# Attention half steps of a decoder kernel reordered: maxima transposed in the next half step, bias additions ahead of the maximum, output projection in odd half steps

## The chip, the cores and the metric

The kernel runs on one core of one Trainium2 chip. The metric is the device time of one execution in microseconds (us); lower is better. A kernel's time is the median of its runs.

## What is computed

The input is `x` of 64 sequences x 128 positions x 256 features, a context `ctx` of the same shape, and a mask of 64 x 128 ones and zeros. Six residual sublayers follow one another, each on the layernorm of the sum so far:

```python
x = x + window_attention(layernorm(x), ...)            # A
x = x + cross_attention_0(layernorm(x), ctx, mask)     # B, its attention
x = x + slot_network(layernorm(x), ...)                # B, beside it
x = x + self_attention_with_bias(layernorm(x), ...)    # D
x = x + cross_attention_1(layernorm(x), ctx, ...)      # E
x = x + bitnet_feed_forward(layernorm(x), ...)         # F
```

What matters here are the three full attentions (B, D and E). Each has 16 heads of 16 features and, for each sequence, computes

```python
scores = einsum('bhqd,bhkd->bhqk', q, k) * scale (+ bias)   # 128 x 128 for each head
p      = softmax(scores, axis=-1)
y      = einsum('bhqk,bhkd->bhqd', p, v)                    # then the output projection
```

In B, `q` and `k` are slices of the normalised `x` and of the context, without a projection, and the mask is applied to queries and keys. In D there is a learned bias for each head, query and key, which is minus infinity where the key comes after the query. In E queries come from `x`, keys and values from `ctx`, all projected. The slot network routes each token to the best 8 of 64 slots (top 8, softmax), averages the tokens of each slot, updates the slots with a gated cell, and reads them back.

## The kernel before

**Stages.** The core runs A, B, D, E, F in turn (B holds the first cross attention and the slot network). `x` stays in SBUF, in 16 groups of GB = 4 sequences ("batches" in the code, 64 in all). The three attentions share one function, `attention_stage`, which is software-pipelined in half steps. Half step `j` belongs to batch `n = j // 2` and half `hf = j % 2`; a half is two of the four row groups of heads, thus 8 heads.

**One batch's way through the half steps.** Since the sums and the weighted values want keys on the partitions, and the maximum wants queries there, the scores of each half are computed twice: once as they are (`first`, for the maximum over keys) and, three half steps later, transposed and with the maximum already taken from the query (`second`, for the exponential).

- `score_burst` (L396, matmuls L409) issues 32 small matmuls when both jobs are there: 16 of `first` and 16 of `second`, alternating, into one PSUM tile `sc` of four banks. This pool has one buffer, so a burst can start only when the last reader of the burst before is done.
- `score_max` (L416) takes the `first` half: in D it adds the bias into an SBUF tile (`sb`, L422), then the negated maximum over keys goes to `negmax` (L424), on DVE.
- `score_exp` (L430) takes the `second` half: in D it adds the bias (`e`, L436, DVE) and takes the exponential of `e`; in B and E the exponential reads the PSUM tile itself (L438, ACT).
- `shift_query` (L442): four PE transposes (L447) of `negmax`, when both halves of the batch are there, then a DVE addition (L451) gives `q2`, the query with the maximum subtracted by way of an extra feature. `second` uses `q2`: half 0 of batch n at half step 2n+3.
- `weigh_values` (L454): 16 matmuls (L459) with the exponentials, copied by ACT (L464). `divide` (L467): four transposes (L471), reciprocal (L474) and product (L478) on DVE. `turn_output` (L483): two transposes (L488) and an ACT copy (L490). `finish_batch` (L493): the output projection (L140) and the addition to `x` by `fin` (L1053 in D and E, L623 in B, DVE).

The loop at the end of `attention_stage` places these: the batch's `weigh_values` at lag 5 from its first half step, `divide` at lag 6, `turn_output` at 7, `finish_batch` at 8, `shift_query` at lag 1. `start(n + 1)` calls the stage's `prep` for the next batch in even half steps. PSUM tiles of all the other steps come from a pool of four buffers (`ps`).

**Around it.** In D and E the projections of the next group (`group_project`) are a generator in nine portions: layernorm; transposes; four portions of two matmuls into q and k (L131, ACT copies L1009); two portions of values (L1020, DVE additions L1025). `advance(g + 1, 2)` in `prep` takes two portions for each batch, in the even half step. In E the layernorm portion also issues the context's DMA on SP's queue. In B `prep` builds padded queries and keys on DVE and POOL and transposes them (L616), and the `tick` of the slot network, called at the end of every half step, takes one portion of `slots_route` or of two `slots_update` generators; a group's routing starts at the half step behind the one in which its last batch is finished.

**Order.** The program is written as one sequence; a scheduler then fixes the order of each engine's instructions, and each engine works through its own list. So where a function stands in the loop influences, but does not alone decide, where its instructions stand on PE, DVE, ACT and POOL.

Of the kernel before, what the change touches and what calls it, by code (L numbers as in the profile page):

```python
# [10 lines left out]
F = mybir.dt.float32  # L11
BF = mybir.dt.bfloat16
AF = mybir.ActivationFunctionType
ALU = mybir.AluOpType
AX = mybir.AxisListType
# [4 lines left out]
S = 128  # L20
WIN = 7
SLOTS = 64
GB = 4
# [389 lines left out]
    return t  # L413


def score_max(k, pool, t, job, bias_s):  # L416
    nc = k.nc
    b, hf = job
    src = t[:, 0:2, :]
    if bias_s is not None:  # L420
        sb = pool.tile([S, 2, 512], F, tag="sb", name="sb")
        nc.vector.tensor_tensor(sb, src, bias_s[:, hf * 2 : hf * 2 + 2, :], ALU.add)  # L422
        src = sb
    nc.vector.tensor_reduce(  # L424
        b.lay.extra(b.nm, hf * 2),
        src.rearrange("p r (c m) -> p r c m", m=S), AX.X, ALU.max, negate=True,
    )


def score_exp(k, pool, w1, t, job, bias_t):  # L430
    nc = k.nc
    b, hf = job
    src = t[:, 2:4, :]
    e = (w1 if hf else pool).tile([S, 2, 512], F, tag=f"e{hf}", name=f"e{hf}")
    if bias_t is not None:
        nc.vector.tensor_tensor(e, src, bias_t[:, hf * 2 : hf * 2 + 2, :], ALU.add)  # L436
        src = e
    nc.scalar.activation(e, src, AF.Exp)  # L438
    b.e[hf] = e


def shift_query(k, pool, b):  # L442
# [11 lines left out]
def weigh_values(k, pool, b):  # L454
    nc = k.nc
    av = psum(k)
    for c in range(4):
        for r in range(4):
            nc.tensor.matmul(  # L459
                av[32 * r : 32 * r + 32, c * S : (c + 1) * S], b.va[:, b.lay.head(c, r), :],  # L460
                b.e[r // 2][:, r % 2, c * S : (c + 1) * S], start=True, stop=True,
            )
    b.avs = pool.tile([128, 4, S], F, tag="avs", name="avs")
    nc.scalar.copy(b.avs, av.rearrange("p (c l) -> p c l", l=S))  # L464


def divide(k, pool, b):  # L467
    nc = k.nc
    tv = psum(k)
    for c in range(4):  # L470
        nc.tensor.transpose(tv[:, c * S : (c + 1) * S], b.avs[:, c, :], k.ident)  # L471
    avv = tv.rearrange("p (h i) -> p h i", i=32)
    rec = pool.tile([S, H], F, tag="rec", name="rec")
    nc.vector.reciprocal(rec, avv[:, :, 16])  # L474
    if b.row_scale is not None:
        nc.vector.tensor_scalar(rec, rec, b.row_scale, None, ALU.mult)
    b.ao = pool.tile([S, H, DH], F, tag="ao", name="ao")
    nc.vector.tensor_tensor(  # L478
        b.ao, avv[:, :, 0:16], rec.unsqueeze(2).to_broadcast([S, H, DH]), ALU.mult
    )  # L480
# [12 lines left out]
def finish_batch(k, b, wo):  # L493
    py = psum(k)
    out_project(k, py[:, 0:D], b.aT, wo)
    b.fin(py[:, 0:D])


def attention_stage(k, pool, w1, prep, wo, lay, bias_s=None, bias_t=None, tick=None):

    nms = []
    for i in range(2):
        t = w1.tile([S, lay.size], F, name=f"negmax{i}")
        k.nc.gpsimd.memset(t, 0.0)
        nms.append(t)
    bs = {}  # L510

    def start(n):
        b = bs[n] = prep(n)
        b.lay = lay
        b.nm = nms[n % 2]
        b.e = [None, None]

    def at(j, lag):
        n, odd = divmod(j - lag, 2)
        return bs.get(n) if not odd else None  # L520

    start(0)
    for j in range(2 * k.NB + 9):
        n, hf = divmod(j, 2)
        first = (bs[n], hf) if n < k.NB else None
        m, mf = divmod(j - 3, 2)
        second = (bs[m], mf) if 0 <= m < k.NB else None
        if first or second:
            t = score_burst(k, first, second)
            if first:  # L530
                score_max(k, w1, t, first, bias_s)
            if second:
                score_exp(k, pool, w1, t, second, bias_t)
        if at(j, 5):
            weigh_values(k, pool, at(j, 5))
        if at(j, 6):
            divide(k, pool, at(j, 6))
        if at(j, 7):
            turn_output(k, pool, at(j, 7))
        if at(j, 8):  # L540
            finish_batch(k, bs.pop((j - 8) // 2), wo)
        if hf == 0 and n + 1 < k.NB:
            start(n + 1)
        if hf == 1 and n < k.NB:
            shift_query(k, pool, bs[n])
        if tick is not None:
            tick(j)

# [421 lines left out]
def stage_attn(k, w, cross, bias=None):  # L970
    nc = k.nc
    pre = "we" if cross else "wd"
    bias_t, bias_s = bias if bias is not None else (None, None)
    with k.tc.tile_pool(name=pre, bufs=2) as wp, k.tc.tile_pool(name=pre + "1", bufs=1) as w1:
        vas = []
        for i in range(2):
            va = w1.tile([S, GB, H, 32], F, name=f"{pre}va{i}")
            nc.gpsimd.memset(va, 0.0)
            nc.gpsimd.memset(va[:, :, :, 16:17], 1.0)
            vas.append(va)  # L980
        proj, pending = {}, {}

        def group_project(g):

            xn = w1.tile([S, GB, D], F, tag="xn", name="xn")
            cx = load_group(k, w1, g) if cross else None
            layernorm(k, wp, g, xn)
            nc.gpsimd.tensor_tensor(  # L988
                k.x[g], k.x[g], w.bo.unsqueeze(1).to_broadcast([S, GB, D]), ALU.add
            )  # L990
            yield
            xnT = w1.tile([128, 2, GB * S], F, tag="xnT", name="xnT")
            transpose_group(k, xn, xnT)
            if cross:
                kvT = w1.tile([128, 2, GB * S], F, tag="kvT", name="kvT")
                transpose_group(k, cx, kvT)
            else:
                kvT = xnT
            yield
            qt = wp.tile([128, 4, GB * S], F, tag="qt", name="qt")  # L1000
            kt = wp.tile([128, 4, GB * S], F, tag="kt", name="kt")
            for dst, wt, src, sc, bi in (
                (qt, w.wq, xnT, w.parq, w.bq), (kt, w.wk, kvT, w.par, w.bk)
            ):
                for cc in range(2):
                    p = psum(k)
                    project(k, p, wt, cc * 128, 128, src, 0, GB * S)
                    for par in range(2):
                        nc.scalar.activation(  # L1009
                            dst[:, 2 * cc + par], p, AF.Identity,  # L1010
                            scale=sc[:, par : par + 1], bias=bi[:, cc, par : par + 1],
                        )
                    yield
            va = vas[g % 2]
            for b2 in range(2):
                p = psum(k)
                for j in range(2):
                    b = b2 * 2 + j
                    for kc in range(2):
                        nc.tensor.matmul(  # L1020
                            p[:, j * D : (j + 1) * D], kvT[:, kc, b * S : (b + 1) * S],
                            w.wv[:, kc, :], start=(kc == 0), stop=(kc == 1),
                        )
                for j in range(2):
                    nc.vector.tensor_tensor(  # L1025
                        va[:, b2 * 2 + j, :, 0:DH],
                        p[:, j * D : (j + 1) * D].rearrange("p (h d) -> p h d", d=DH),
                        w.bv.rearrange("p (h d) -> p h d", d=DH), ALU.add,
                    )
                if b2 == 0:  # L1030
                    yield
            proj[g] = qt, kt, va

        def advance(g, parts):
            for _ in range(parts):
                if g in pending and next(pending[g], pending) is pending:
                    del pending[g]

        def prep(bi):
            g, b = divmod(bi, GB)  # L1040
            if bi == 0:
                pending[0] = group_project(0)
            if b == 0:
                advance(g, 9)
                if g + 1 < k.G:
                    pending[g + 1] = group_project(g + 1)
            advance(g + 1, 2)
            qt, kt, va = proj[g]
            t = Batch()
            t.qt, t.kt = qt[:, :, b * S : (b + 1) * S], kt[:, :, b * S : (b + 1) * S]  # L1050
            t.va, t.row_scale = va[:, b], None
            xb = k.x[g][:, b, :]
            t.fin = lambda y: nc.vector.tensor_tensor(xb, y, xb, ALU.add)  # L1053
            return t

        attention_stage(k, wp, w1, prep, w.wo, Heads(True), bias_s, bias_t)

# [375 lines left out]
```

## Time and profile before

| | |
|---|---|
| three runs (us) | 3784.18, 3775.18, 3778.06; median 3778.06 |
| the profiled execution (us) | 3773.99, its span 3772.2 |
| mean granted PE clock | 0.89 |
| PE busy | 2993.5 us, 79% of the span |
| DVE busy | 2562.4 us, 68% |
| ACT busy | 1274.6 us, 34% |
| POOL busy | 1058.7 us, 28% |
| chain that ended last | PE 47%, DVE 32%, POOL 10%, ACT 7%, issue 3%, DMA 1% |

By the timeline stage A takes the first 608 us, B 614 to 1560 (with the preparation of D's bias to about 1655), D 1658 to 2420, E 2430 to 3100 and F the rest. "Busy" counts neither register work nor the issue of DMAs. PE is TensorE's matmuls, PEld its weight loads, DVE the vector engine, ACT the scalar engine, POOL the general engine, SP the queue that starts most DMAs. In the chain of waits, a line `PE x <- DVE y: a, b, c` means that PE stood before x for a us in all, b times, the longest c, and that y released it. In the chain that ended last a line gives start, duration, engine, output and line.

### The profile page before, as it was taken

Reading aid. Unit: us, or ns where it says so; the run is one execution under the profiler, and the core shown is the slowest. Engines: PE = TensorE matmul, PEld = TensorE weight load, DVE = VectorE, ACT = ScalarE, POOL = GpSimd, SP = SyncE. Lnnn points to the kernel's source line nnn. Section 1 sums busy time; section 2 is a strip of 40 time slices with the busy share of each in tenths; the row PEclk is TensorE's granted clock in tenths of the full one; section 3 lists DMA queues with packets and bytes.
Section 4 is the critical chain, followed back from the end, with each engine's and each line's share of the span. In section 5 each row is a group of like instructions: output and inputs, shape, how many; then the busy total and the mean of one; then the engine's idle time right before and its main releaser. Section 6 shows DMA issues by size and latency. Waiting matters only on the chain.

```text
span 3772.2 us, 65003 instructions
## 1 busy us (share of the span) xinstructions
PE 2993.5 (79%) x27764; PEld 1928.4 (51%) x27764; DVE 2562.4 (68%) x4875; ACT 1274.6 (34%) x1883; POOL 1058.7 (28%) x1048
## 2 busy tenths in 40 slices
PE   4888885887888888688888888888889976667776
PEld 1333333655656556456666666566666753333333
DVE  5878766656656555567888777755555547887766
ACT  1111111434333343323333333244444433332332
POOL 3555543423333232220000000110000014434334
PEclk9999986999889999779999999799999997888887
DMA  5000000000000000000000000000000000000000
GB/s 185 1 1 0 1 1 17 13 13 7 13 7 13 12 7 1 1 15 1 1 1 1 1 1 1 13 17 13 18 13 13 13 1 6 12 17 12 12 17 17
DMA packets 40815, 48.06 MB, mean 13 GB/s; under 512 B 4448, under 2 KB 37616, under 8 KB 40272
## 3 DMA queue, kind: packets, MB, share of 16 engines
q1 hardware_dynamic: 39872, 42.17, 3.5%
q8 instruction: 219, 3.59, 0.4%
q0 software_dynamic: 656, 1.75, 0.2%
q14 instruction: 68, 0.56, 0.0%
HBM read 35.52 MB, written 8.39 MB: 12 GB/s over the span
## 4 chain that ended last, share of the span: by engine, by line
PE 47%; DVE 32%; POOL 10%; ACT 7%; issue 3%; DMA 1%; SPq 0%; DVEq 0%; POOLq 0%; ACTq 0%
PE sc L409 10%; PE ps L131 9%; PE ps L140 7%; DVE negmax L424 6%; PE cv L1172 4%; DVE uq L1224 4%; PE ps L1020 3%; DVE sb L422 3%; PE ps L447 3%; ACT e L438 3%; DVE e L436 2%; POOL pr L260 2%; DVE pv L318 2%; PE ps L459 2%; DVE oT L322 2%
## 5 line engine op out<-in xcount | busy, mean ns | idle before, releaser
L409 PE MATMUL sc<-kt,qt 32*128 32x128 f32 x6144 | 549.0, 305 | 161.1 <-DVE e L436 104.7
L409 PEld LDWEIGHTS sc<-kt,qt 32*128 32x128 f32 x6144 | 446.9, 202 | 318.9 <-issue 196.1
L409 PE MATMUL sc<-q,kt 32*128 32x128 f32 x6144 | 545.0, 305 | 2.0 <-DVE e L436 1.6
L424 DVE TENSOR_REDUCE negmax<-sc 128x8 f32<-128x1024 f32 x256 | 312.9, 1222 | 267.1 <-PE sc L409 267.1
L409 PEld LDWEIGHTS sc<-q,kt 32*128 32x128 f32 x6144 | 443.1, 202 | 13.2 <-issue 10.0
L438 ACT ACTIVATE e<-sc 128x1024 f32<-128x1024 f32 x256 | 262.7, 1026 | 396.1 <-DVE negmax L424 391.3
L1172 PE MATMUL cv<-hp,taps 128*128 128x512 f32 x480 | 260.1, 692 | 87.7 <-DVE hp L1162 82.5
L260 POOL TENSOR_TENSOR pr<-pad,qt 128x896 f32<-128x896 f32 x128 | 243.9, 1940 | 211.3 <-ACT pad L247 211.2
L447 PE MATMUL ps<-ident,negmax 128*128 128x128 f32 x768 | 135.9, 304 | 178.8 <-DVE negmax L424 176.9
L451 DVE TENSOR_TENSOR q<-ps,qt 128x512 f32<-128x512 f32 x192 | 132.6, 691 | 148.7 <-PE ps L447 142.1
L438 ACT ACTIVATE e<-e 128x1024 f32<-128x1024 f32 x128 | 135.3, 1057 | 286.1 <-DVE e L436 286.1
L464 ACT COPY avs<-ps 128x512 f32<-128x512 f32 x192 | 112.0, 584 | 343.1 <-PE ps L459 343.1
L422 DVE TENSOR_TENSOR sb<-sc,bias_s 128x1024 f32<-128x1024 f32 x128 | 156.5, 1223 | 96.9 <-PE sc L409 96.9
L1172 PEld LDWEIGHTS cv<-hp,taps 128*128 128x128 f32 x480 | 103.9, 224 | 218.7 <-issue 112.0
L447 PEld LDWEIGHTS ps<-ident,negmax 128*128 128x128 f32 x768 | 88.6, 151 | 218.0 <-issue 140.0
L318 DVE TENSOR_TENSOR pv<-sc,pad 128x896 f32<-128x896 f32 x128 | 137.1, 1083 | 91.1 <-PE sc L312 91.1
L988 POOL TENSOR_TENSOR x<-x,t_d_bo 128x1024 f32<-128x1024 f32 x16 | 37.6, 2352 | 561.6 <-DVE xn L107 561.6
L988 POOL TENSOR_TENSOR x<-x,t_e_bo 128x1024 f32<-128x1024 f32 x16 | 37.5, 2346 | 489.6 <-DVE xn L107 489.6
L1223 POOL TENSOR_TENSOR hs<-hs,s2b 128x512 f32<-128x512 f32 x128 | 171.2, 1373 | 9.9 <-ACT s2b L1215 9.9
L1224 DVE TENSOR_SCALAR uq<-hs 128x512 bf16<-128x512 f32 x128 | 152.9, 1227 | 10.2 <-POOL hs L1223 10.2
L436 DVE TENSOR_TENSOR e<-sc,bias_t 128x1024 f32<-128x1024 f32 x128 | 155.5, 1215 | 5.2 <-PE sc L409 5.1
L424 DVE TENSOR_REDUCE negmax<-sb 128x8 f32<-128x1024 f32 x128 | 155.0, 1211 | 0.1
(328 smaller groups left out, 6531.0 us busy)
## 6 DMA issues: line engine op xcount, KB each, us to landing
cx<-in_ctx_dram SPq DMA_DIRECT2D x32, 512.0 KB, 3.8
x<-in_x_dram SPq DMA_DIRECT2D x16, 512.0 KB, 8.8
out_dram<-x SPq DMA_DIRECT2D x16, 512.0 KB, 2.9
t_g_w<-in_g_w_dram SPq DMA_DIRECT2D x2, 1024.0 KB, 6.1
t_c_wih<-in_c_wih_dram SPq DMA_DIRECT2D x1, 768.0 KB, 4.7
t_c_whh<-in_c_whh_dram SPq DMA_DIRECT2D x1, 768.0 KB, 7.5
t_a_cw<-in_a_cw_dram SPq DMA_DIRECT2D x1, 448.0 KB, 10.6
t_c_bih<-in_c_bih_dram POOLq DMA_DIRECT2D x1, 384.0 KB, 4.9
```

The source lines that it names most:

```text
L131: k.nc.tensor.matmul(out, w[:, kc, c0 : c0 + cn], rhsT[:, kc, n0 : n0 + n], start=(kc == 0), stop=(kc == 1),)
L140: k.nc.tensor.matmul(out, aT[:, kc, :], w[:, kc, :], start=(kc == 0), stop=(kc == 1))
L260: k.nc.gpsimd.tensor_tensor(pr[:, c], shift_windows(t.kt, b, c), t.qt[:, c, b, :].unsqueeze(1).to_broadcast([128, WIN, S]), ALU.mult,)
L318: nc.vector.tensor_tensor(pv, bc[th][:, :, 0 : WIN * 64].rearrange("p c (l w) -> p c l w", w=WIN), shift_windows2(t.vt, b, th), ALU.mult,)
L409: k.nc.tensor.matmul(t[:, side * 2 + rr, c * S : (c + 1) * S], st[rows, c, :], mv[rows, c, :], start=True, stop=True,)
L422: nc.vector.tensor_tensor(sb, src, bias_s[:, hf * 2 : hf * 2 + 2, :], ALU.add)
L424: nc.vector.tensor_reduce(b.lay.extra(b.nm, hf * 2), src.rearrange("p r (c m) -> p r c m", m=S), AX.X, ALU.max, negate=True,)
L436: nc.vector.tensor_tensor(e, src, bias_t[:, hf * 2 : hf * 2 + 2, :], ALU.add)
L438: nc.scalar.activation(e, src, AF.Exp)
L447: nc.tensor.transpose(pt[:, c * S : (c + 1) * S], b.nm[:, b.lay.base[c] : b.lay.base[c] + S], k.ident)
L1172: nc.tensor.matmul(pc, w.taps[:, CONV_PE.index(j), t, :], hp[:, :, t : t + S], start=(t == 0), stop=(t == 2),)
L1224: nc.vector.tensor_scalar(uq[:, j], hs[:, j], MAGIC, MAGIC, ALU.add, ALU.subtract)
```

## The change

The functions `score_max` and `score_exp` become one, `score_halves`. It issues the bias addition of `first` (`sb`), then for `second` the bias addition (`e`) and the exponential, and the maximum of `first` last. In `attention_stage` the steps are sorted into even and odd half steps: `shift_query` moves from half step 2n+1 to 2n+2, `finish_batch` from lag 8 to lag 9, and `weigh_values`, `turn_output` and `finish_batch` now stand in odd half steps, `divide` and `start` in even ones, with `shift_query` ahead of `divide`. The loop has one half step more. In D and E `prep` takes one portion of the next group's projections for each batch (in the even half step), and a new `tick` takes one in the odd half step.

```diff
-def score_max(k, pool, t, job, bias_s):
...
-def score_exp(k, pool, w1, t, job, bias_t):
...
+def score_halves(k, pool, w1, t, first, second, bias_s, bias_t):
+    nc = k.nc
     src = t[:, 0:2, :]
+    if first and bias_s is not None:
+        hf = first[1]
+        sb = w1.tile([S, 2, 512], F, tag="sb", name="sb")
         nc.vector.tensor_tensor(sb, src, bias_s[:, hf * 2 : hf * 2 + 2, :], ALU.add)
         src = sb
+    if second:
+        b, hf = second
+        e = (w1 if hf else pool).tile([S, 2, 512], F, tag=f"e{hf}", name=f"e{hf}")
+        if bias_t is not None:
+            nc.vector.tensor_tensor(e, t[:, 2:4, :], bias_t[:, hf * 2 : hf * 2 + 2, :], ALU.add)
+            nc.scalar.activation(e, e, AF.Exp)
+        else:
+            nc.scalar.activation(e, t[:, 2:4, :], AF.Exp)
+        b.e[hf] = e
+    if first:
+        b, hf = first
+        nc.vector.tensor_reduce(
+            b.lay.extra(b.nm, hf * 2), src.rearrange("p r (c m) -> p r c m", m=S),
+            AX.X, ALU.max, negate=True,
+        )
...
-    for j in range(2 * k.NB + 9):
+    for j in range(2 * k.NB + 10):
...
-            if first:
-                score_max(k, w1, t, first, bias_s)
-            if second:
-                score_exp(k, pool, w1, t, second, bias_t)
-        if at(j, 5):
-            weigh_values(k, pool, at(j, 5))
-        if at(j, 6):
-            divide(k, pool, at(j, 6))
-        if at(j, 7):
-            turn_output(k, pool, at(j, 7))
-        if at(j, 8):
-            finish_batch(k, bs.pop((j - 8) // 2), wo)
-        if hf == 0 and n + 1 < k.NB:
-            start(n + 1)
-        if hf == 1 and n < k.NB:
-            shift_query(k, pool, bs[n])
+            score_halves(k, pool, w1, t, first, second, bias_s, bias_t)
+        if hf == 0:
+            if at(j, 2):
+                shift_query(k, pool, at(j, 2))
+            if at(j, 6):
+                divide(k, pool, at(j, 6))
+            if n + 1 < k.NB:
+                start(n + 1)
+        else:
+            if at(j, 5):
+                weigh_values(k, pool, at(j, 5))
+            if at(j, 7):
+                turn_output(k, pool, at(j, 7))
+            if at(j, 9):
+                finish_batch(k, bs.pop((j - 9) // 2), wo)
         if tick is not None:
             tick(j)
...
-            advance(g + 1, 2)
+            advance(g + 1, 1)
...
-        attention_stage(k, wp, w1, prep, w.wo, Heads(True), bias_s, bias_t)
+        def tick(j):
+            if j % 2 and j // 2 + 1 < k.NB:
+                advance((j // 2 + 1) // GB + 1, 1)
+
+        attention_stage(k, wp, w1, prep, w.wo, Heads(True), bias_s, bias_t, tick)
```

More of the change, by code (lines that the diff above doesn't have):

```diff
@@ L413, in score_burst @@
     return t
-def score_max(k, pool, t, job, bias_s):
+def score_halves(k, pool, w1, t, first, second, bias_s, bias_t):
     nc = k.nc
-    b, hf = job
     src = t[:, 0:2, :]
-    if bias_s is not None:
-        sb = pool.tile([S, 2, 512], F, tag="sb", name="sb")
+    if first and bias_s is not None:
+        hf = first[1]
+        sb = w1.tile([S, 2, 512], F, tag="sb", name="sb")
         nc.vector.tensor_tensor(sb, src, bias_s[:, hf * 2 : hf * 2 + 2, :], ALU.add)
         src = sb
[L424 to L427, printed above, removed]
-def score_exp(k, pool, w1, t, job, bias_t):
[L431 to L439, printed above, removed]
+    if second:
[13 more added lines that the diff above has]
+        )
 def shift_query(k, pool, b):
```

## The prediction

> **What bounds the kernel now.** I read the windows by stage first. The change touches three attention stages: the first cross attention with the slot network (614 to 1560 us), the self attention with bias (1658 to 2420), the second cross attention (2430 to 3100). I call them B, D and E; columns are length, then busy time (and count) of PE, PEld, DVE, ACT, POOL, then clock and DMA.
>
> ```profile
> 608.00:1560.00 952.00, 758.59 (x8598) 555.42 (x8596) 563.97 (x1488) 371.23 (x610) 331.82 (x468) 0.90 0.03 10
> 1665.00:2420.00 755.00, 623.07 (x7538) 456.58 (x7536) 594.31 (x849) 278.59 (x383) 41.75 (x24) 0.91 0.01 1
> 2420.00:3110.00 690.00, 600.23 (x7854) 440.92 (x7852) 389.62 (x732) 290.58 (x419) 74.02 (x63) 0.95 0.04 14
> ```
>
> No engine is full in any stage: PE 80 to 87%, DVE 79% in D. So a chain decides, and the waits of each stage (who <- whom: us, times, longest) say which. B, then D, then E:
>
> ```profile
> ACT e L438 <- DVE negmax L424: 199.0, 83, 5.0
> ...
> PE ps L447 <- DVE negmax L424: 103.9, 48, 3.4
> ```
> ```profile
> PE sc L409 <- DVE e L436: 106.4, 66, 3.3
> PE ps L447 <- DVE negmax L424: 22.3, 61, 0.4
> ```
> ```profile
> ACT e L438 <- DVE negmax L424: 192.3, 71, 4.6
> ...
> PE ps L447 <- DVE negmax L424: 50.6, 20, 4.4
> ```
>
> PE stands before the transposes of the maxima (L447) for 177 us over the three stages, and before the score burst (L409) mostly in D. The only score tile is free again when its last reader is done. In D the chain that ended last shows one batch:
>
> ```profile
> 2007.18 1.15 PE sc L409 x32
> 2008.33 0.02 issue
> 2008.35 1.22 DVE sb L422
> 2009.57 1.13 DVE e L436
> 2010.70 1.14 DVE negmax L424
> 2011.84 0.14 issue
> 2011.98 0.63 PE ps L447 x4
> 2012.61 1.58 PE sc L409 x20
> 2014.19 1.04 PE ps L471 x4
> ```
>
> Two things are to be seen. The second burst is cut by L447, which waits for the maximum (the timeline: 12 instructions from 2010.85, then nothing until 2011.98). And the order on DVE is already sb, e, negmax. In B the same link follows the slot network's DVE work:
>
> ```profile
> 1057.91 1.15 DVE negmax L424
> 1059.19 0.63 PE ps L447 x4
> 1059.82 2.97 PE ps L131 x4
> 1062.79 1.54 PE sc L409 x32
> ```
>
> **Bias additions ahead of the maximum.** Worth nothing in D: the rows above have that order before the change. Where there is no bias (B, E), the exponential goes first and the maximum behind it. In the timeline of E ACT starts 0.09 us after DVE ends on the same tile (2701.11, 2701.21), and in the built order the maximum now waits for ACT instead. Exponential 1.03 us and maximum 1.23 us stay in line, 2.6 us with their gaps: 0 by this row. [...]
>
> **Transposes one half step later, in D.** The built order after an even burst (end = 0) is, on PE, L447, L471, half a projection, the first matmul of the odd burst, most of L459, the rest of the burst; on DVE sb, e, negmax, query addition. DVE operations start 1.14 apart: e is ready at 2.4, its exponential (1.06) at 3.6, so 0.85 us of L459 ends at 4.5. The shifted query now has no slack: the transposes are done early, its addition (0.69) follows the maximum and ends at 4.15. That is under 4.5, so PE decides; the burst rest ends at 5.55. Odd half step: PE has 0.2 of L459, 0.44 (L488), 0.96 (L140) and half a projection, 1.77: 3.4 us, against 2.5 for e; with the burst 4.55. A batch is 5.55 + 4.55 = 10.1, before 11.18 (distance of the query additions L451 where nothing disturbs). Four batches: -4.3. Against it, the layernorm block (copy 0.68, normalising 1.37, aggregates 0.37) now stands ahead of sb and of the query addition: I get 1.65 us on the path, before 0.3 (11.47 against 11.18): +1.35. So -3.0 per group of four batches, 13 groups, and about -8 us in the last three, which have fewer projections: **D -46 us**.
>
> **Projections in halves.** The same instructions and DMAs in twice as many portions, in the even and in the odd half step. The half in the odd step covers the 2.5 us for which PE waits now (used above). In E it puts two ACT copies (2 x 0.72) ahead of each exponential: tile free 4.05 us after the burst's start instead of 3.75. PE's own even half is 1.10 + 0.47 + 0.50 + 1.77 = 3.84, odd 1.10 + 1.01 + 0.50 + 0.96 + 1.77 = 5.34: a batch is 4.05 + 5.34 = 9.4, against 9.35 now. The layernorm block of E costs about 4 us of idle PE in both orders (4.36 before L447 at 2695.86 now; then 3.8 before a burst). The context DMAs (3.8 us to landing) keep a half step of lead. **E 0**, between -20 and +25.
>
> **B.** A group takes some 60 us, in four pieces that move. (1) After the slot update: from the odd burst's end (1054.43) to the even burst (1062.72) 8.3 us: DVE chain, maximum, L447, L131 in line. After: L447 is elsewhere and L131 goes ahead of the maximum; PE has 1.08 + 0.44 + 0.96 + 3.1 = 5.6, DVE 4.8: -2.7. (2) Layernorm of the slots: the even burst no longer waits for it, the following odd one does (L623, statistics, POOL 1.04, four xn, query addition, maximum): 8.6 + 0.9 (a PSUM buffer that L478 frees late) against 11.2 (1032.90 to 1044.14): -1.7. (3) Two of the slot matmuls move ahead of the burst: about 10 us against 12.3 (1062.72 to 1075.05): -2.4. (4) Top-8 and softmax: ten small DVE operations now precede the maximum, where six did: +1.5, and the query addition behind four additions to x: +0.85. Sum -4.4 per group, 13 groups -57, the three without slots -5: **B -62 us**. The bounds of this unknown are 0 (each piece hits another wait) and -104 (all of L447's idle time in B).
>
> **Output projection in odd half steps** (L140 from the even half): 0.96 us, counted above; its DVE addition follows the maximum, where DVE has 0.8 us to spare in D. If that cover is gone, it costs up to 0.36 x 64 = 23 us.
>
> The profiled execution took 3773.99 us (span 3772.2, 1.8 around it); -62 - 46 gives 3666. The median of the runs is 4 us above the profiled one: **3670**.
>
> **Clock.** Row: after 4.36 us of idle PE the burst at 2697.73 takes 2.09 us, others 1.17; and in D the burst rest at 2012.54 takes 1.65 against 0.94, though PE was never idle for over 1.2 us there. It recurs twice per group (12.69 against 11.18, +1.5). I keep as many slow stretches as now. [...] What fewer gaps would give is the second rival.
>
> **Rivals.**
> - B stays pinned by the slot network's DVE and POOL chain (for: 85.6 and 53.1 us of waits between them; against: L447's 104 us): D alone, 3778 - 46 = 3732, with some of B 3725. Chance 0.20.
> - Denser PE keeps its full clock: D's 1.5 us twice for 16 groups is 48 at most, half of it 24; B has some 190 us at half clock, a third of the 95 lost is 32: 3670 - 56 = 3614. For: less idle; against: D's slow stretches follow no long gap. Chance 0.10.
> - Slower: the query addition, now needed one half step after its transposes instead of two, is late. [...] It decides from 1.1 us of added wait per batch in D (that eats the gain) on. For: no slack; against: in D I have 4.15 under 4.5. Chance 0.14.
> - It does nothing, the built order being much the same: against it, L447 stands elsewhere in all three stages. Chance 0.03.
>
> **Numbers.** Forecast 0.53, its own range 3625 to 3715. The whole range reaches from the clock rival to past the pinned B with E's +25 (3757): 3600 to 3765, leaving out the slower case, the no-change case and the tails. 0.2% (7.5 us) is about what a measurement can tell from no change. Faster 0.82 (forecast, most of the pinned case, clock), same 0.04, slower 0.14.
>
> **What would show it.** Right: query additions in D some 10.1 us apart, no idle PE before L447, groups of B near 56 us, E's length unchanged. Wrong: PE idle before the odd burst on "DVE q" (slower rival), B groups still at 60 (pinned), or fewer slow stretches in D (clock).

## The result, and the profile after

The changed kernel takes 3564.97 us (median of 4 runs, 3556.39 to 3570.27), the kernel before 3776.62 (median of 4, 3771.56 to 3784.18). The ratio is 0.9436, 95% interval 0.941 to 0.9461. The sign was forecast, the size was not: 212 us came, 106 were forecast, and 3565 lies below the range. The profiled execution after took 3556.39 us (span 3554.6), the shortest of its four.

The windows by stage, each from the first query addition (L451) of B, D and E to its last, so that both kernels do the same work in them (about the same count of matmuls). Before:

```profile
638.70:1508.90 870.20, 709.38 (x8295) 523.07 (x8296) 522.41 (x1367) 350.12 (x574) 288.16 (x407) 0.91 0.03 9
1666.30:2406.30 740.00, 608.11 (x7444) 445.83 (x7444) 588.43 (x839) 274.67 (x378) 41.75 (x24) 0.92 0.01 1
2458.30:3081.70 623.40, 558.67 (x7554) 412.80 (x7552) 349.23 (x603) 272.20 (x392) 41.66 (x24) 0.96 0.04 13
```

After:

```profile
628.30:1414.40 786.10, 667.75 (x8299) 505.21 (x8297) 518.44 (x1367) 355.54 (x576) 291.20 (x406) 0.94 0.03 10
1566.70:2225.00 658.30, 588.04 (x7450) 415.50 (x7450) 588.83 (x843) 273.92 (x380) 41.78 (x24) 0.96 0.01 2
2268.90:2866.60 597.70, 545.94 (x7557) 408.89 (x7558) 342.23 (x603) 277.04 (x395) 41.68 (x24) 0.95 0.04 13
```

The second number is the length, the third PE's busy time. Both fall, and that is the first thing to see:

| stage | length | PE busy | the rest (PE not busy) | forecast |
|---|---|---|---|---|
| B | -84 | -42 | -42 | -62 |
| D | -82 | -20 | -62 | -46 |
| E | -26 | -13 | -13 | 0 |
| sum | -192 | -75 | -117 | -108 |

In the sum PE's idle time fell by about what was forecast. That is partly luck: by stage it missed by 20, 16 and 13 us, and these cancel in part. The same matmuls also took 75 us less, for which the forecast had nothing. Outside these windows the one profile is some 26 us shorter. Of these, 8 us lie between D and E, where the stages drain and fill. The rest lies ahead of B, between B and D and at the end, where nearly the same code runs and the 16 other profiles of this study scatter by as much (B's first query addition lies between 632.2 and 642.6 us in them, at 628.3 after the change, although stage A is untouched).

Who PE waits for now, in these three windows (B, D, E; who <- whom: us, times, longest):

```profile
PE sc L409 <- DVE negmax L436: 39.9, 59, 4.3
PE ps L140 <- ACT giT L802: 25.6, 13, 2.4
...
PE ps L794 <- DVE q L451: 17.5, 13, 1.3
```
```profile
PE sc L409 <- DVE e L429: 55.1, 40, 3.8
PE ps L459 <- ACT e L430: 12.6, 32, 0.5
```
```profile
PE sc L409 <- DVE negmax L436: 51.5, 36, 3.8
```

In B, `giT` and L794 belong to the slot network (L140 is a helper that it shares). The transposes of the maxima (L447), for which PE stood 177 us before, are in none of these lists. What is left in D is the wait for the second bias addition, 106 us before. One batch of D in the chain that ended last shows the new cadence:

```profile
1904.08 1.23 DVE sb L423
1905.31 1.14 DVE e L429
1906.45 0.02 issue
1906.47 1.07 ACT e L430
1907.54 0.04 issue
1907.58 0.86 PE ps L459 x22
1908.44 1.10 PE sc L409 x30
1909.53 0.35 PE ps L459 x6
1909.88 0.37 PE ps L488 x2
1910.25 0.86 PE ps L140 x4
1911.12 1.72 PE ps L131 x4
1912.83 1.15 PE sc L409 x32
```

The even half step runs over DVE and the exponential (burst's end to burst's end 5.5 us, forecast 5.55), the odd one over PE alone (4.4, forecast 4.55): L488, L140 and half a projection lie where PE stood idle. (A group's projections are eight portions, not nine: two for each of its four batches.) Query additions come 9.92 us apart, before 11.18, forecast 10.1.

### The profile page after: what moved, and what is told of

It is laid out like the page before. It is cut to its first block, busy times and chain, and to the rows that moved or that the text cites. A ratio compares the mean times of both kernels' runs of the same rounds, so it can differ in the third digit from the quotient of the medians.

```text
span 3554.6 us, 64872 instructions
## 1 busy us (share of the span) xinstructions
PE 2895.9 (81%) x27764; PEld 1859.2 (52%) x27764; DVE 2562.0 (72%) x4875; ACT 1278.2 (36%) x1883; POOL 1064.4 (30%) x1048
## 4 chain that ended last, share of the span: by engine, by line
PE 41%; DVE 37%; POOL 11%; ACT 7%; issue 3%; DMA 1%; SPq 0%; POOLq 0%; DVEq 0%; ACTq 0%
PE sc L409 10%; PE ps L131 7%; DVE negmax L436 6%; PE ps L140 5%; PE cv L1176 5%; PE ps L459 4%; DVE uq L1228 4%; DVE sb L423 3%; DVE e L429 3%; POOL pr L260 2%; DVE pv L318 2%; DVE oT L322 2%; POOL dg L1122 2%; ACT e L430 2%; POOL ln_rs L100 2%
## 5 line engine op out<-in xcount | busy, mean ns | idle before, releaser
L409 PE MATMUL sc<-kt,qt 32*128 32x128 f32 x6144 | 521.2, 297 | 160.2 <-DVE negmax L436 103.9
L409 PEld LDWEIGHTS sc<-kt,qt 32*128 32x128 f32 x6144 | 426.2, 197 | 339.4 <-DVE negmax L436 156.2
L409 PE MATMUL sc<-q,kt 32*128 32x128 f32 x6144 | 494.7, 297 | 4.9 <-DVE q L451 2.6
L409 PEld LDWEIGHTS sc<-q,kt 32*128 32x128 f32 x6144 | 410.2, 197 | 24.2 <-DVE rec L474 10.8
L260 POOL TENSOR_TENSOR pr<-pad,qt 128x896 f32<-128x896 f32 x128 | 244.0, 1941 | 198.8 <-ACT pad L247 198.6
L451 DVE TENSOR_TENSOR q<-ps,qt 128x512 f32<-128x512 f32 x192 | 131.8, 686 | 155.2 <-PE ps L447 155.2
L97 DVE BATCH_NORM_STATS2 ln_st<-x 128x6 f32<-128x256 f32 x384 | 146.5, 412 | 3.9 <-PE ps L140 2.1
L322 DVE TENSOR_REDUCE oT<-pv 128x128 f32<-128x896 f32 x128 | 136.8, 1081 | 2.1
```

The lines of the kernel that those rows point to most:

```text
L260: k.nc.gpsimd.tensor_tensor(pr[:, c], shift_windows(t.kt, b, c), t.qt[:, c, b, :].unsqueeze(1).to_broadcast([128, WIN, S]), ALU.mult,)
L322: nc.vector.tensor_reduce(oT[:, :, 64 * th : 64 * th + 64], pv, AX.X, ALU.add)
L409: k.nc.tensor.matmul(t[:, side * 2 + rr, c * S : (c + 1) * S], st[rows, c, :], mv[rows, c, :], start=True, stop=True,)
```

## The experiments

Times are medians, each beside the kernel before on the same chip; its medians lie between 3772.6 and 3778.6 us, so a few us between a run and the changed kernel's 3565, which was timed apart from it, say nothing. A table further down has the stages of the runs on single parts.

**One stage at a time.** Only the named stage uses the new `attention_stage` (in D and E with the projection halves), the others the old one.

```diff
-        attention_stage(k, wp, w1, prep, w.wp, Heads(False), tick=slots.tick)
+        attention_stage_old(k, wp, w1, prep, w.wp, Heads(False), tick=slots.tick)   # not B
...
-            advance(g + 1, 1)
+            advance(g + 1, 1 if new else 2)      # new: D or E, or neither
```

> The change in the first cross attention and slot stage (B) alone; D and E as before. If each stage's gain is its own, B goes from some 952 to 868 us (the query additions of B spanned 870 before and 786 after) and the kernel to 3777 - 84 = 3693 us, with stage A unchanged against before. If the 20 us that fell outside the three stages (stage A was 10 us shorter in the profile after) come with B's first half steps, 3677. If B's gain needs the neighbours (earlier weight loads, a shared pool), over 3710.

> The change in the self attention (D) alone. Theory of the cadence: the query additions of D come 9.9 us apart instead of 11.2 and the stage is 82 us shorter: 3695 us. By my forecast for D it would have been 3731. If D's gain were borrowed from what B left behind, over 3720.

> The change in the second cross attention (E) alone. Theory: 26 us shorter (8.9 instead of 9.35 us per batch), 3751 us. My forecast for E was 0: 3777. The sum of the three stages alone against the whole change (213 us) tells whether the stages add up: 84 + 82 + 26 = 192 would leave 21 us for coupling or for scatter of the one profile.

B alone 3681.2 against 3772.6 (ratio 0.9756, 0.973 to 0.9782): -91. D alone 3695.9 (0.9798, 0.9769 to 0.9826): -77. E alone 3748.1 (0.993, 0.9914 to 0.9946): -25. Each stage's gain is its own; the sum, -193, leaves 19 us of the 212. In the profiles D accounts for as much: alone it spans 677.0 us, behind the changed B 658.3, though PE's and DVE's instructions of D stand in the same order in both builds. What differs is the clock: 89 us at half clock against 48. A part of that is the choice of the execution: the profile of D alone is the longest of its four (3708.9 us, median 3695.9), that of the whole change the shortest. In D alone the groups of four batches are 44.3 us long nearly throughout, and both slow stretches come back in each.

**More work on PE, in the kernel before.** This tests the clock by itself.

```diff
 def turn_output(k, pool, b):
...
-    for kc in range(2):
-        nc.tensor.transpose(p[:, kc * S : (kc + 1) * S], aof[:, kc * 128 : (kc + 1) * 128], k.ident)
+    for _ in range(b.fill):      # D: 11 if b == 0 else 5; B and E: 1
+        for kc in range(2):
+            nc.tensor.transpose(
+                p[:, kc * S : (kc + 1) * S], aof[:, kc * 128 : (kc + 1) * 128], k.ident
+            )
```

> The kernel before, with nothing moved: in D the two transposes of turn_output are repeated (5 times, 11 times in the batch beside the layernorm), so that PE is busy in the stretch in which it waits for the second bias addition. PE has more work, no data changes. Theory of the clock: a 3.4 us window in which PE is busy for less than about half gives a window at half clock behind it; with the gap filled D's slow windows fall from 33 to under 12, each is worth about 1.4 us, and D gets 30 us shorter although PE does more: 3747 us. Rival, the slow windows have nothing to do with the idle time: as many as before, and 3777, or up to 20 us more where the added transposes reach the path.

3734.3 against 3772.6, ratio 0.9887 (0.9864 to 0.9909): -38 us, all in D (703.2 against 740.0), with 670 matmuls more there. D's stretches at half clock fall from 33 to 7. The windows show how; first the kernel before, in two pairs of neighbouring 3.41 us windows:

```profile
2009.08:2012.49 3.41, 1.81 (x26) 1.17 (x18) 2.75 (x3) 1.92 (x3) 0.00 (x0) 1.00 0.00 0
2012.49:2015.90 3.41, 3.41 (x29) 2.96 (x28) 2.35 (x3) 0.00 (x0) 0.00 (x0) 0.50 0.00 0
2032.97:2036.38 3.41, 1.29 (x16) 0.97 (x16) 3.38 (x9) 1.06 (x1) 1.81 (x2) 1.00 0.00 0
2036.38:2039.79 3.41, 3.41 (x28) 3.00 (x28) 3.41 (x7) 0.00 (x0) 1.02 (x1) 0.50 0.00 0
```

PE busy is the number behind the length, the clock the third from the end. Busy 1.81 or 1.29 of 3.41 us, and the next window runs at 0.50, although it is full. In the first of these windows no gap of PE is over 1.2 us; the second holds the larger part of a gap of 3.15 us (2031.62 to 2034.77), once per group. The kernel with the added transposes over a whole D:

```profile
1669.10:2372.30 703.20, 637.85 (x8114) 483.05 (x8114) 587.33 (x839) 273.11 (x378) 41.95 (x24) 0.98 0.01 2
```

The clock is 0.98 instead of 0.92. In both profiles, before and after the change, every record of the clock is 1.00 or 0.50, and all of them begin on one grid of 3.413 us. In D before the change (from 1655 us on, with the preparation of its bias), all 14 windows of this grid with PE busy under half were followed by one at half clock, 18 of 23 with 50 to 60%, and 8 of 186 above that. In B it is 30 of 30 under half and 5 of 15 with 50 to 60%, in E 10 of 10 and 1 of 7. So in these stages half clock went with the busy share of the window before: all 54 windows under half were followed by it, 24 of 45 with 50 to 60%; one long gap was not needed, since the first window above has none over 1.2 us.

**One part undone at a time**, from the changed kernel.

```diff
-            if at(j, 2):                              # transposes back in the odd half step
-                shift_query(k, pool, at(j, 2))
+            if at(j, 1):
+                shift_query(k, pool, at(j, 1))
...
-            advance(g + 1, 1)                         # projections whole, no tick
+            advance(g + 1, 2)
...
-            if at(j, 9):                              # output projection in the even half step
-                finish_batch(k, bs.pop((j - 9) // 2), wo)
+            if at(j, 8):
+                finish_batch(k, bs.pop((j - 8) // 2), wo)
...
-            score_halves(k, pool, w1, t, first, second, bias_s, bias_t)    # old order
+            score_max(...); score_exp(...)
```

> The changed kernel with one part undone: the transposes of the maxima stand again at the end of the odd half step 2n+1, where the second maximum has just been asked for. Theory: this part took PE's wait for the maximum away (177 us before, 0.3 us left); undone, PE waits for the maximum again, some 0.6 to 1 us per batch in D and E and several us per group in B, and some 100 of the 213 us are lost: 3665 us. Rival, the wait was only moved and the cadence comes from the projection halves: under 3600.

3801.5 against 3778.6, ratio 1.006 (1.0038 to 1.0082): all of the gain is lost, and 23 us more. My 3665 was far off. PE's waits are back at the transposes, in E for 52.1 us, in D for 18.5, and in B for:

```profile
PE ps L447 <- DVE negmax L436: 81.7, 61, 4.0
```

> The changed kernel with the projections of D and E taken again two portions at a time in the even half step. Theory: in D the odd half step loses the 1.8 us of projection that cover the wait for the second bias addition (2.5 us), so 0.9 us per batch come back and fewer but longer idle stretches bring slow windows: D +60, E (where PE is busy nearly throughout) +5, B 0: 3630 us. Rival, the query addition sets D's half steps and not PE: D unchanged, 3565.

3581.0, ratio 0.9475 (0.9452 to 0.9497): 16 us lost, not 65. D 665.4, E 609.6.

> The changed kernel with the output projection again in the even half step (lag 8 instead of 9). It takes 0.96 us of PE from the odd half step, in which PE had 3.4 us against the 2.5 us of the second bias addition in D, and gives them to the even one. Theory: D's even half step is set by the exponential and PE's order, so +0.3 us per batch there, +20 us; E 0, B between -10 and +10: 3585 us. Rival, DVE's addition to x no longer stands behind the maximum and the layernorm of the slots comes half a step earlier: B gains 20, 3550.

3578.5, ratio 0.9475 (0.9454 to 0.9496): 14 us lost, near the 20 expected, but by luck, since it is made up otherwise: B +17, D +18, E -25.

> The changed kernel with the old order of the two halves (maximum asked for ahead of the second bias addition and the exponential). In D DVE stood in the order sb, e, negmax before the change too, so 0 there; in B and E the exponential and the maximum read one PSUM tile in line in either order, 0 by that. Theory: within 10 us of the changed kernel, 3565. Rival, the order of the exponential decides in E: 0.4 us per batch, 26 us, 3590.

3638.9, ratio 0.9632 (0.9612 to 0.9653): 74 us lost. D is unchanged (659.2), as expected; E +7; B +62 (847.8). In B the burst now waits for the exponential:

```profile
PE sc L409 <- ACT e L438: 88.5, 47, 3.5
```

Against 39.9 us for the maximum after the change. In the chain of this run a burst of B follows a maximum of 1.15 and an exponential of 1.02 to 1.03 us in line. In B DVE comes late to the maximum, since the slot network is queued ahead of it; with the new order the exponential is done by then (in the changed kernel's timeline one starts at 1041.48, the maximum of the same tile at 1044.46), with the old one it still follows. B is at half clock for 207 us here, 88 in the changed kernel: the longer waits and the clock come together, and how much is each's was not separated.

**Parts added to the kernel before.** The first has only the moved transposes, the second also the new order, the third only the projection halves.

```diff
+        if at(j, 2):                       # runs 1 and 2
+            shift_query(k, pool, at(j, 2))
         if at(j, 5):
             weigh_values(k, pool, at(j, 5))
...
-        if hf == 1 and n < k.NB:
-            shift_query(k, pool, bs[n])
...
-            advance(g + 1, 2)              # run 3, with the changed kernel's tick
+            advance(g + 1, 1)
```

> The kernel before with one part only: the transposes of the maxima at the start of the even half step 2n+2; all else as before. With this part undone the changed kernel lost all its gain, with each other part undone 14 to 74 us of it. If the transposes are the cause and the others add to it, before - 213 + 16 + 14 + 74 = 109 us shorter than before, about 3668. Rival, the parts need each other (the transposes only pay where the sorted half steps give PE other work behind the burst): within 30 us of before.

> The kernel before with two parts: the transposes at the start of the even half step, and the exponential ahead of the maximum; projections whole and the output projection in the even half step as before. If parts add up, 213 - 16 - 14 = 183 us shorter than before, about 3594; the step from the run with the transposes alone is then 74 us, nearly all of it in B. If order and halves need each other, it stays near that run.

> The kernel before with the projections of D and E in halves, one portion in each half step, and nothing else. My prediction took the projection half in the odd half step as what covers PE's wait in D. If the halves pay by themselves, D is 20 to 50 us shorter: 3725 to 3755. If they pay only where the transposes have left the odd half step (the four parts together without the transposes gave 3801), D is within 20 us of before and E up to 50 us longer (there two ACT copies stand ahead of each exponential): 3775 to 3830.

3705.3 (ratio 0.9819, 0.9795 to 0.9844), 3719.5 (0.9856, 0.9832 to 0.9879) and 3782.7 (1.0017, 1.0006 to 1.0028). The transposes alone give 69 us, a third, and nothing in E, where PE still waits 48.9 us before L447 (49.2 before). The order alone behind them costs 14 us in all: B -16, D 0, E +35, where PE now waits 110 us for the maximum, which stands last. The halves alone are not faster: D +33, more than the 20 that I had allowed, with 147 us at half clock against 119, and E -14, where I had expected E to be longer. So the parts need one another, and the table says which:

| run | B | D | E |
|---|---|---|---|
| before | 870.2 | 740.0 | 623.4 |
| transposes moved | 816.5 | 726.3 | 623.1 |
| halves only | 870.1 | 773.2 | 609.8 |
| transposes, order | 800.6 | 726.1 | 658.0 |
| all but the output projection | 802.7 | 676.0 | 572.5 |
| all but the halves | 782.9 | 665.4 | 609.6 |
| all but the order | 847.8 | 659.2 | 604.8 |
| all but the transposes | 876.2 | 720.9 | 674.6 |
| all (the change) | 786.1 | 658.3 | 597.7 |

(us from the first to the last L451 of the stage, one profile each; stages with the old code repeat within 2.2 us over all runs, the changed B spans 780 to 791, the changed D 656 to 677 with the clock.) In D either the output projection or a projection half in the odd half step takes D from 726 to 665 or 676, and both together to 658: one piece of PE work there covers most of the wait, so undoing only one of them costs little.

**Two tries at the layernorm of E.** After the change PE waits 3.8 us once per group in E. The timeline there, engine by engine:

```profile
2576.01 2.34 POOL L987 TENSOR_TENSOR x<-x,t_e_bo 128x1024 f32<-128x1024 f32 x1 [37.43 <-DVE xn L107]
2576.38 2.00 DVE L99 TENSOR_SCALAR ln_ve<-ln_mv 128x4 f32<-128x4 f32 x1
...
2578.29 1.39 DVE L97 BATCH_NORM_STATS2 ln_st<-x 128x6 f32<-128x256 f32 x4
...
2579.60 0.67 DVE L451 TENSOR_TENSOR q<-ps,qt 128x512 f32<-128x512 f32 x1
...
2581.46 0.58 PE L409 MATMUL sc<-kt,qt 32*128 32x128 f32 x1 [3.84 <-DVE negmax L436]
```

Four elements per partition take DVE 2.00 us, and this ends with POOL's addition (at 2578.38 and 2578.35). The first try moves this operation to POOL; the second fills the wait with repeated transposes.

```diff
-    nc.vector.tensor_scalar(ve, mv[:, :, 1], 1e-5, None, ALU.add)
+    (eng or nc.vector).tensor_scalar(ve, mv[:, :, 1], 1e-5, None, ALU.add)   # eng: POOL in E
...
-    for c in range(4):                # second try, in divide
-        nc.tensor.transpose(tv[:, c * S : (c + 1) * S], b.avs[:, c, :], k.ident)
+    for _ in range(b.fill):           # batch 1 of a group: 5 in D, 8 in E; else 1
+        for c in range(4):
+            nc.tensor.transpose(tv[:, c * S : (c + 1) * S], b.avs[:, c, :], k.ident)
```

> The changed kernel, with one operation of the layernorm of E (variance plus epsilon, 128x4, L99) on POOL instead of DVE. On DVE it took 2.00 us in E, ending with POOL's 2.35 us addition of the bias to x (L987), against 0.10 to 0.17 us where POOL is idle; the query addition and the maximum stand behind it, and PE waits 3.8 us. Theory: DVE's operation is held for as long as POOL's runs, and moving it saves 2.0 us in each of some 12 groups and takes PE's idle stretch under half a clock window: -24 to -50 us against the changed kernel, 3520 to 3541. Rival, the next operation on DVE (statistics, L97) is held in its place: 3565.

3519.0 against 3774.2, ratio 0.9324 (0.9303 to 0.9346), 46 us less than the changed kernel; by the profiles E is 35 us shorter. The same place now:

```profile
2592.01 2.35 POOL L987 TENSOR_TENSOR x<-x,t_e_bo 128x1024 f32<-128x1024 f32 x1 [34.53 <-DVE xn L107]
2592.38 1.41 DVE L97 BATCH_NORM_STATS2 ln_st<-x 128x6 f32<-128x256 f32 x4
...
2594.33 0.23 POOL L99 TENSOR_SCALAR ln_ve<-ln_mv 128x4 f32<-128x4 f32 x1
...
2595.57 0.37 PE L409 MATMUL sc<-kt,qt 32*128 32x128 f32 x1 [1.94 <-DVE negmax L436]
```

The four statistics (L97) take 1.41 us beside POOL's addition, and 1.39 us behind it in the changed kernel, PE waits 1.94 instead of 3.84 us, and a matmul of the next burst takes 0.37 instead of 0.58 us, at a clock of 1.00 here and 0.50 in the changed kernel. Why L99 takes 2.00 us beside that addition while L97 takes no longer, no trace shows.

> The changed kernel with idle PE filled: in the one batch per group whose even half step has the layernorm on DVE, the four transposes of divide are repeated (5 times in D, 8 in E), no data changes, nothing is moved. In E PE waits 3.8 us there and then runs 6.8 us at half clock (burst 2.09 us instead of 1.17, weighted values 1.94 instead of 1.08, transposes and output projection 1.5 times as long). Theory of the clock: the slow window goes, 2 to 3 us per group, E -30 and D -10: 3525 us. Rival, the wait behind it absorbs what the clock gives, or the filler delays the copies on ACT: 3565 or more.

3569.9 (ratio 0.9461, 0.9428 to 0.9493): no gain. In E the clock did what was expected (58 us at half clock to 0, E 10 us shorter); D came out at 669.9 instead of 658.3, with 58 us at half clock, and B 5 us longer without being touched.

**E's output projection back in the even half step**, alone and with L99 on POOL.

```diff
-            if at(j, 9):
+            if not late and at(j, 8):     # even half step; late: B and D
+                finish_batch(k, bs.pop((j - 8) // 2), wo)
...
+            if late and at(j, 9):
```

> The changed kernel, with the output projection of E alone again in the even half step (lag 8); B and D as in the changed kernel. The run with it back everywhere had 572 us between E's first and last query addition against 598, and lost in D and B. Theory: in E PE has no wait in the odd half step to cover, and L140 in the even one covers 0.9 us of the wait behind the layernorm, so the odd place costs E 25 us: 3540. Rival, E's 25 us were the clock's phase in that one profile: 3565.

> The version that the runs point to: the changed kernel with E's output projection in the even half step and E's small layernorm operation (L99) on POOL. The two save in the same wait behind the layernorm (3.8 us, of which 2.0 by the one and 0.9 by the other), so if both fit: 3565 - 46 - 25 = 3494; if the wait is gone after the first, 3519.

3537.9 (ratio 0.9359, 0.9345 to 0.9372), 27 us less than the changed kernel: in E the odd place costs, and with the even one E is at half clock for 17 us instead of 58. Both together 3510.8 (0.9288, 0.9257 to 0.932), the fastest version and between the 3494 and 3519 expected, E 541.8 us and never at half clock. Against L99 on POOL alone (E 563.0) the profile has 21 us less in E, the medians only 8, within the spread of both (3499.1 to 3523.6 and 3514.7 to 3524.7).

## Why the prediction was right in sign and short by half

- **What bounds, and the moved transposes: right.** PE's wait for the maximum is gone, and without this part all the gain is lost.
- **The steps of D: right in structure.** Even half step 5.5 for 5.55, odd 4.4 for 4.55, the layernorm's cost +1.6 for +1.35 (11.51 against 9.92 in the group's third batch). The odd half step, lower than forecast, is worth 0.15 x 64 = 10 us.
- **"I keep as many slow stretches as now": the step that failed.** The time at half clock fell from 159 to 88 us in B and from 119 to 48 in D, 142 us together; at the 0.50 of the records that is worth up to 71. An estimate by the run with the added transposes, where 97 us less at half clock (119 to 22) went with 37 us in D, is 54, 27 in each stage. In D, 46 forecast, this 27 and the 10 above make 83, for 82 measured. How much of the change's own gain is the clock's was not separated by a run. In E the time at half clock did not fall (51 to 58 us). The prediction noticed that D's slow stretch followed no gap over 1.2 us and took that as a sign that it wouldn't go with the gaps. It overlooked the second stretch of each group, which follows the gap of 3.15 us. The windows and the added transposes show the reverse of its reading: the window with gaps of at most 1.2 us (PE busy 1.81 of 3.41 us, 53%) was followed by one at 0.50, just as the one with most of the long gap was (1.29 of 3.41). The clock rival (3614) had this mechanism, with 56 us for it and a chance of 0.10.
- **"Stay in line: 0 by this row", for the order: wrong in B.** It was read off E, at a place where the one follows the other on the same tile. Where DVE comes late, as in B with the slot network, the exponential no longer stands behind it, and undoing the order costs 62 us in B, of which a part may be the clock. In D the 0 holds. In E it depends on the other parts: undoing the order in the changed kernel costs 7 us, adding it to the moved transposes alone costs 35.
- **E at 0: wrong, -26.** These are mis-sized terms. The odd half step was put at 5.34 us and takes 5.07, since the 0.50 for L488 was read off the old order, where L447 behind it waited for the maximum; without that wait it is 0.27. The even one takes 3.85 for 4.05. A batch is 8.92 for 9.4. The layernorm's 3.8 us before a burst came as forecast (3.84). Of PE's 13 us less busy time in E, 8 are the output projection (L140, 73.3 to 65.3 us). Left in E are the odd place of the output projection and L99's 2.00 us beside POOL.
- **B's pieces: -62 forecast, -84 in the profile, -91 alone.** Half of it is PE busy time. Full groups of B take 50 to 55 us, forecast near 56. The four pieces were not separated one by one.
- **The slower rival** (a late query addition): PE's waits in D and E have none for L451. In B there are 17.5 us, 13 waits of at most 1.3, before L794: the rival's mechanism, but small. In B and E the chain does run through it behind layernorm blocks, as in the timeline above; that cost is part of what the third batch of a group shows.

## What to carry to other kernels

Before pricing a cut in idle time on PE, list the granted clock beside PE's busy share, in windows as long as the grid of the clock's records (3.41 us here). In the kernel before, each of the 54 windows under half busy was followed by one at half clock, so idle time there had a second cost, and filling the gaps took most of it away in D: with the added transposes the time at half clock fell from 119 to 22 us and D got 37 us shorter. When two parts cover the same wait (here the output projection and the projection half), undoing one says little; undo and add, stage by stage. A duration read as a distance between two instructions may hold a wait that the change removes: take it from a place where the follower is not waiting.

## What was not expected of the hardware

- Work added to PE, with nothing moved, made the kernel 38 us faster; D's granted clock was 0.98 instead of 0.92.
- Groups whose slow stretches come back in each were whole multiples of the grid in three cases: D's groups before the change were 47.8 us long, 14 times 3.413; in D alone 44.3, 13 times; in E after the change 41.0, 12 times. In E before the change, at 41.6 to 43.0, they were not. The same instruction order ran D in 658 or 677 us, with 48 or 89 us at half clock. That the slow stretch itself draws the group to a multiple is argued from these lengths, not tested.
- A 128x4 operation on DVE took 2.00 us beside an addition on POOL, and 0.10 to 0.17 us where POOL was idle; in stage A it took up to 1.92 us beside POOL's products (L260). On POOL behind the addition it took 0.23.
